# Attention and FP4 feed-forward on one core: the queue's products as two halves of 64 rows between the scores

## The chip, the core and the metric

The kernel runs on one core of a Trainium2 chip. The core has a matrix engine (TensorE, "PE" in the profile, with its weight loads shown apart as "PEld"), VectorE ("DVE"), ScalarE ("ACT"), GpSimd ("POOL") and SyncE ("SP"), whose queue issues nearly all of the transfers here. TensorE writes only to PSUM, which has eight banks of 512 float32 columns for each of its 128 partitions. The metric is the device time of one execution in microseconds (us), as a median of runs.

## The reference

One transformer layer with layer norms behind its two blocks, on x of 4 x 2048 x 256 in float32. Attention has 16 heads of 16 elements. The feed-forward block quantizes its inputs and weights to FP4 (E2M1) in blocks of 16 and has 704 hidden units.

```python
q, k, v = (split_heads(x @ W.T) for W in (Wq, Wk, Wv))
attn = softmax(einsum('bhld,bhmd->bhlm', q, k) * SCALE, axis=-1)
x = layernorm(x + merge_heads(einsum('bhlm,bhmd->bhld', attn, v)) @ Wo.T)

def fp4_quant_dequant(x):            # blocks of 16 along the last dimension
    scale = maximum(max(abs(xb)) / 6.0, 1e-12)
    idx = searchsorted(_MID, abs(xb / scale))
    return _GRID[idx] * sign(xb) * scale

def fp4_linear(x, w):
    return einsum('bsk,nk->bsn', fp4_quant_dequant(x), fp4_quant_dequant(w))

h = silu(fp4_linear(x, w_gate)) * fp4_linear(x, w_up)
x = layernorm(x + fp4_linear(h, w_down))
```

## The kernel before

**Steps and periods.** A step is one batch, one block of 512 queries and one group of four heads: 4 x 4 x 4 = 64 steps. Each step has 16 key tiles of 128 keys, and the main loop at the end of `block_kernel` runs one *period* for each key tile of each step, 1024 in all. A period does four heads' worth of three things on TensorE:

- `maxima` (scores for the row maxima, 20 periods ahead of the exponentials): two pairs of score matmuls into `pm`, each pair a tile of two banks. VectorE reduces each pair in one instruction of 1024 elements per partition (L397).
- `exponentials`: two pairs of score matmuls into `pe`, one bank for each head; ScalarE takes the exponential of each (L431).
- `values` (two periods behind the exponentials): four matmuls of 32 output columns each into the bank `av`, one for each head.

A score contracts 62 or 64 rows. The q and k of a pair of heads lie on partitions 0 to 63 (`j` = 0) and 64 to 127 (`j` = 1), so the two matmuls of a pair use different rows of the array. The order within a period is: both pairs of `maxima`, the first pair of `exponentials`, `values`, the second pair of `exponentials`, and then the period's part of the queue.

**The queue.** All other work is written as generators that yield after each part. `period` takes one such part for each period (`urgent` ones first): projections (`project`), the turning of maxima into rows (`max_rows`), the division by the sums (`normalize`), and for each block of 512 rows a `chain` through `feed_forward`: `residual`, the gate and up products (`gated`), transposes (`turned`) and `down`. A part is a group of matmuls on all 128 rows into one bank from `psum`, and its eviction by ScalarE. By shape there are four kinds: four transposes of 128 x 128; products of two contraction chunks with up to 256 output columns (pq, pv, py) or with 352 (pg, pu); and `down`'s products of six chunks (the last of 64 rows) with 128 columns (pz). A float32 matmul call stands in the profile as two matmul records, a score or a transpose as one.

**PSUM.** `ps_m` holds two tiles of two banks for `pm`; `ps_x` holds three banks that `pe` and the queue's parts share; one bank is `av`.

**Helpers.** `later` and `take_due` put VectorE's and GpSimd's work a given number of periods later. `fp4` quantizes a tile in two such steps: reduce, scale, reciprocal and the first multiplication at once, then the rounding. `layer_norm` issues all of its instructions at once. `load_k` fills a ring of 20 key tiles (two for each 512 keys of a step), 28 periods ahead of the exponentials and 8 ahead of the maxima.

**Order.** TensorE's instructions are kept in the order of the code (L134 and L137 are the helpers that record it). Every engine works through its instructions as written, each waiting for the semaphores of what it needs.

Of the kernel before, what the change touches and what calls it, by code (L numbers as in the profile page):

```python
# [30 lines left out]
F32 = mybir.dt.float32  # L32
# [21 lines left out]
LAG = 2  # L54
LEAST = 300.0
# [9 lines left out]
EXPONENT = 0x7F800000  # L65

# [7 lines left out]
def block_kernel(  # L74
# [24 lines left out]
    ps_m = ctx.enter_context(tc.tile_pool(name="ps_m", bufs=2, space=PSUM))  # L99
    ps_av = ctx.enter_context(tc.tile_pool(name="ps_av", bufs=1, space=PSUM))  # L100
    ps_x = ctx.enter_context(tc.tile_pool(name="ps_x", bufs=3, space=PSUM))


    banks = {"n": 0, "more": False}

    def psum(name):
        banks["n"] += 1
        if banks["more"] and banks["n"] % 2:
            return ps_m.tile([P, 2, 512], F32, tag="pm", name=name)[:, 0, :]
        return ps_x.tile([P, 512], F32, tag="px", name=name)  # L110
# [5 lines left out]
    def later(periods, step, rest=0):  # L116

        state = {"done": None}
        due.append((clock["now"] + periods, step, state))
        return lambda: state["done"] is not None and clock["now"] >= state["done"] + rest  # L120

    def take_due():
        clock["now"] += 1
        for _ in range(len(due)):
            at, step, state = due.popleft()
            if at > clock["now"]:
                due.append((at, step, state))
                continue
            step()
            state["done"] = clock["now"]  # L130


    def matmul(*args, **kw):
        tc.keep_in_program_order(nc.tensor.matmul(*args, **kw))  # L134

    def transpose(*args):
        tc.keep_in_program_order(nc.tensor.transpose(*args))  # L137
# [7 lines left out]
    def fp4(pool, t, tag, gain=1.0, engine=None):  # L145

        p, nb, _ = t.shape
        amax = pool.tile([p, nb], F32, tag="amax" + tag, name="amax")
        nc.vector.tensor_reduce(amax, t, AX.X, ALU.max, apply_absolute_value=True)  # L149
        sc = pool.tile([p, nb], F32, tag="sc" + tag, name="sc")  # L150
        nc.vector.tensor_scalar(sc, amax, gain / 6.0, 1e-12, ALU.mult, ALU.max)
        rs = pool.tile([p, nb], F32, tag="rs" + tag, name="rs")
        nc.vector.reciprocal(rs, sc)
        engine = engine or nc.gpsimd
        engine.tensor_scalar(rs, rs, gain * TIES_DOWN, 1.0, ALU.mult, ALU.mult)
        xn = pool.tile([p, nb, FB], F32, tag="xn" + tag, name="xn", bufs=3 if tag else 2)
        engine.tensor_tensor(xn, t, rs.unsqueeze(2).to_broadcast([p, nb, FB]), ALU.mult)

        def rounded():
            m = pool.tile([p, nb, FB], F32, tag="m" + tag, name="m", bufs=1)  # L160
            nc.vector.tensor_single_scalar(m.bitcast(I32), xn.bitcast(I32), EXPONENT, ALU.bitwise_and)
            nc.vector.tensor_scalar(m, m, 1.0, ROUND, ALU.max, ALU.mult)  # L162
            engine.tensor_tensor(xn, xn, m, ALU.add)  # L163
            engine.tensor_tensor(xn, xn, m, ALU.subtract)  # L164
            engine.tensor_tensor(xn, xn, sc.unsqueeze(2).to_broadcast([p, nb, FB]), ALU.mult)  # L165

        return xn, later(1, rounded, 4 if tag == "" else 2)
# [37 lines left out]
    for name, w in (("wk", wk), ("wq", wq), ("wv", wv)):  # L205
        loaded[name] = p2.tile([P, KC, D], F32, tag="xnh", name=name, bufs=3)
# [7 lines left out]
    for name, dst in (("wk", wkT), ("wq", wqT), ("wv", wvT)):  # L214
        for kc in range(KC):
            pt = psum("ptw")
            for n in range(KC):
                transpose(pt[:, n * P : (n + 1) * P], loaded[name][:, n, kc * P : (kc + 1) * P], ident)
            if name == "wv":
# [9 lines left out]

    RF = FF // 8  # L230

    def prepare():
# [5 lines left out]
        for kc in range(KC):  # L238
            for n in range(KC):
                at = (kc * KC + n) * P  # L240
                transpose(pt[:, at : at + P], raw[:, n, kc * P : (kc + 1) * P], ident)
        nc.scalar.copy(woT.rearrange("p k n -> p (k n)"), pt)
        yield 500

        def load(w, i):
            if w is w_down:
                t = p2.tile([P, FF], F32, tag="wl", name="wl", bufs=1)
                nc.sync.dma_start(t, w[i * P : (i + 1) * P, :])
                return fp4(p2, t.rearrange("p (b f) -> p b f", f=FB), "h")
            t = p2.tile([RF, 2, D], F32, tag="wl", name="wl", bufs=1)  # L250
            nc.sync.dma_start(t, w[2 * i * RF : 2 * (i + 1) * RF, :].rearrange("(c p) k -> p c k", p=RF))
            return fp4(p2, t.rearrange("p c (b f) -> p (c b) f", f=FB), "")

        def transposed(w, i, q, done):
            while not done():
                yield LEAST
            if w is w_down:
                q = q.rearrange("p b f -> p (b f)")
                for c0 in range(0, NFC, 4):
                    pt = psum("ptw")  # L260
                    for c in range(c0, min(c0 + 4, NFC)):
                        n = min(P, FF - c * P)
                        at = (c - c0) * P
                        transpose(pt[:n, at : at + P], q[:, c * P : c * P + n], ident)
                        nc.scalar.copy(wdT[:n, c, i * P : (i + 1) * P], pt[:n, at : at + P])
                return
            q = q.rearrange("p (c b) f -> p c (b f)", c=2)
            pt = psum("ptw")
            for kc in range(KC):
                for c in range(2):  # L270
                    at = (2 * kc + c) * RF
                    transpose(pt[:, at : at + RF], q[:, c, kc * P : (kc + 1) * P], ident[:RF, :RF])
# [3 lines left out]
            )  # L276

        pieces = [(w, i) for w in (w_gate, w_up) for i in range(4)] + [(w_down, i) for i in range(KC)]
        q = load(*pieces[0])
        yield 1  # L280
        for piece, after in zip(pieces, pieces[1:] + [None]):
# [3 lines left out]
            yield 500  # L285

    def weave(main, other, k):

        for cost in main:
            yield cost  # L290
            for _ in range(k if cost else 0):
                cost = next(other, None)
                if cost is None:
                    break
                yield cost
# [4 lines left out]
    def project(b, tb, what):  # L300
# [7 lines left out]
        for kc in range(KC):  # L308
            pt = psum("ptx")
            for t in range(QT):  # L310
                transpose(pt[:, t * P : (t + 1) * P], xb[:, t, kc * P : (kc + 1) * P], ident)
            nc.scalar.copy(xT[:, kc, :], pt)
            yield 600
        for name, c in [(w[0], int(w[1])) for w in what if w != "v"]:
# [3 lines left out]
            for half in range(2):  # L318
                cols = slice(half * QB // 2, (half + 1) * QB // 2)
                pq = psum("pq")[:, : QB // 2]  # L320
                for kc in range(KC):
                    matmul(pq, w[:, kc, c * P : (c + 1) * P], xT[:, kc, cols], start=(kc == 0), stop=(kc == KC - 1))
                nc.scalar.copy(hi[:, cols], pq)
                nc.gpsimd.tensor_tensor(lo[:, cols], read(pq), hi[:, cols].bitcast(F32), ALU.subtract)
                yield 900
# [7 lines left out]
        for t in range(QT if "v" in what else 0):  # L333
            v = vt[t // 2]
            pv = psum("pv")
            for kc in range(KC):
                matmul(
                    pv[:, :D], xT[:, kc, t * P : (t + 1) * P], wvT[:, kc, :], start=(kc == 0), stop=(kc == KC - 1)
                )
            src = pv[:, :D].rearrange("p (g i j d) -> p g i j d", g=NG, i=NP, j=2)  # L340
            for j in range(2):
                nc.scalar.copy(v[:, :, t % 2, :, 2 * j * DH : (2 * j + 1) * DH], src[:, :, :, j, :])
            if t % 2:
                t0 = tb * QT + t - 1
                for g in range(NG):
                    nc.sync.dma_start(vx[b % 2][g, :, t0 : t0 + 2, :], v[:, g].rearrange("p t i c -> p t (i c)"))
            if t == QT - 1:
                projected.add((b, tb, "v"))
            yield 900
# [15 lines left out]
    def load_k(s, kb):  # L365
        b, qb, g = steps[s]
        for i in range(NP):
            c, h = divmod(g * HG + i * 2, NC)
            k = p1.tile([P, QB], F32R, tag="k", name="k", bufs=20)
# [12 lines left out]
    def maxima(s, n, i):  # L382

        if n == 0 and i == 0:
            mx_sb[s] = p2.tile([P, QT, HG, NQB], F32, tag="mx", name="mx")
        kb, t = n // QT, n % QT
        pm = ps_m.tile([P, 2, QB], F32, tag="pm", name="pm")
        for j in range(2):
# [386 lines left out]
```

## Time and profile before

The three runs took 3696.54, 3698.85 and 3699.21 us (median 3698.85). The profiled execution took 3695.37 us, with a span of 3693.6 us from its first to its last instruction; its mean granted TensorE clock was 0.982.

| what | busy us | share of the span | instructions |
|---|---|---|---|
| TensorE matmuls (PE) | 3540.7 | 96% | 21396 |
| TensorE weight loads (PEld) | 1602.0 | 43% | 21396 |
| VectorE (DVE) | 2805.0 | 76% | 3250 |
| ScalarE (ACT) | 2694.0 | 73% | 5452 |
| GpSimd (POOL) | 1293.4 | 35% | 1542 |

"Busy" is the time in which at least one instruction of the engine was under way, so a TensorE that is busy is not one that has both halves of its rows at work. The 16 DMA engines moved 334.18 MB at 90 GB/s on average. The first group of `values` starts at 125.6 us and the last at 3598.4 us; the periods of the main loop lie between, the preparation before, and the last block's feed-forward behind.

A row of the timeline gives the start and the time from the first start to the last end of a run of like instructions, both in us; `x4` counts instructions, and brackets show idle time and what ended it. A row of a group gives busy time and the mean of one in ns, then the idle time before them. Start-to-start times in the timeline are the safer reading for matmuls, because their ends are modelled.

### The profile page before, as it was taken

The page shows a single profiled execution, that of the slowest core. Times are in us where ns is not written, and L with a number is a line of the kernel's source. Part 1 is how long each engine was busy: PE and PEld are TensorE (multiplying, and loading weights), DVE is VectorE, ACT ScalarE, POOL GpSimd, SP SyncE. Part 2 cuts the span into 40 slices and gives each one's busy share as a digit, 9 for nine tenths or more (in the row PEclk, how much of TensorE's full clock was granted, in tenths as well). Part 3 has the DMA queues.
Part 4 walks back from the last instruction along what each step waited for, and adds up shares of the span by engine and source line. Part 5 has one row for each costly group of instructions (what it writes and reads, how often), then busy time and mean ns, then how long its engine had stood idle before and what let it go on. Part 6 is the DMA issues. An engine that isn't in the chain of part 4 may idle for free.

```text
span 3693.6 us, 57860 instructions
## 1 busy us (share of the span) xinstructions
PE 3540.7 (96%) x21396; PEld 1602.0 (43%) x21396; DVE 2805.0 (76%) x3250; ACT 2694.0 (73%) x5452; POOL 1293.4 (35%) x1542
## 2 busy tenths in 40 slices
PE   5889999999999999999999999999999999999995
PEld 4433444444444444444444444444443434444343
DVE  3777777787787877878787787778778788878834
ACT  2667777777777777777777777777777777777772
POOL 0331432424243242423424243342424325241425
PEclk8899999999999999999999999999999999999997
DMA  6643333223232332323323232322322221222100
GB/s 217 188 137 117 93 91 105 81 85 115 68 114 84 94 94 85 109 70 109 95 78 106 85 97 88 97 89 74 113 75 63 75 79 57 75 68 86 47 7 6
DMA packets 197954, 334.18 MB, mean 90 GB/s; under 512 B 26024, under 2 KB 75560, under 8 KB 197672
## 3 DMA queue, kind: packets, MB, share of 16 engines
q1 hardware_dynamic: 196280, 329.16, 29.2%
q8 instruction: 171, 2.80, 0.3%
q10 hardware_dynamic: 1392, 1.31, 0.1%
q14 instruction: 111, 0.91, 0.1%
HBM read 242.81 MB, written 86.51 MB: 89 GB/s over the span
## 4 chain that ended last, share of the span: by engine, by line
PE 82%; DVE 11%; DMA 2%; POOL 2%; SPq 1%; issue 1%; ACT 1%; ACTq 0%; POOLq 0%; DVEq 0%
PE av L134 24%; PE pe L134 18%; PE pm L134 16%; DVE mx L397 8%; PE pz L134 5%; PE pg L134 5%; PE pu L134 5%; PE pq L134 3%; PE pth L137 1%; PE pv L134 1%; PE pa L137 1%; PE py L134 1%; PE pn L137 1%; DMA k<-kx 1%; DMA xb<-in_L_attn_x_dram 1%; DVE amax L149 1%
## 5 line engine op out<-in xcount | busy, mean ns | idle before, releaser
L397 DVE TENSOR_REDUCE mx<-pm 128x2 f32<-128x1024 f32 x2048 | 2407.9, 1217 | 706.8 <-PE pm L134 702.5
L431 ACT ACTIVATE e<-pe 128x512 f32<-128x512 f32 x4096 | 2217.9, 595 | 671.2 <-PE pe L134 666.0
L134 PE MATMUL av<-e,v 128*32 128x512 f32 x8192 | 1098.3, 608 | 0.0
L134 PE MATMUL pe<-q,k 64*128 64x512 f32 x4096 | 1037.2, 456 | 4.8 <-ACT e L431 4.4
L134 PEld LDWEIGHTS pe<-q,k 64*128 64x128 f32 x4096 | 476.4, 185 | 969.0 <-ACT e L431 855.7
L134 PE MATMUL pm<-k,q 62*128 62x512 f32 x4096 | 803.8, 448 | 60.0 <-DVE mx L397 53.0
L134 PEld LDWEIGHTS pm<-k,q 62*128 62x128 f32 x4096 | 347.0, 186 | 373.2 <-issue 178.6
L134 PEld LDWEIGHTS av<-e,v 128*32 128x32 f32 x8192 | 162.2, 108 | 332.2 <-issue 314.1
L537 POOL TENSOR_TENSOR a<-a,g 128x352 f32<-128x352 f32 x124 | 116.4, 939 | 499.5 <-ACT a L536 499.5
L582 POOL TENSOR_TENSOR x<-x,read 128x128 f32<-128x128 f32 x128 | 58.9, 460 | 493.6 <-ACT read L142 493.6
L134 PE MATMUL pz<-wdT,hT 128*128 128x128 f32 (+1 forms) x1536 | 230.0, 292 | 0.0
L163 POOL TENSOR_TENSOR xn<-xn,m 128x704 f32<-128x704 f32 (+2 forms) x104 | 159.5, 1534 | 157.7 <-DVE m L162 139.0
L134 PEld LDWEIGHTS pz<-wdT,hT 128*128 128x128 f32 (+1 forms) x1536 | 191.0, 191 | 45.5 <-ACT e L431 18.2
L551 POOL TENSOR_TENSOR h<-a,u 128x352 f32<-128x352 f32 x124 | 116.2, 937 | 226.7 <-ACT u L550 224.4
L134 PE MATMUL pg<-wgT,xqT 128*128 128x352 f32 x512 | 187.4, 489 | 0.0
L513 POOL TENSOR_TENSOR x<-x,read 128x256 f32<-128x256 f32 x64 | 46.7, 730 | 400.2 <-ACT read L142 399.9
L134 PE MATMUL pu<-wuT,xqT 128*128 128x352 f32 x512 | 186.1, 486 | 0.0
L164 POOL TENSOR_TENSOR xn<-xn,m 128x704 f32<-128x704 f32 (+2 forms) x104 | 159.8, 1536 | 5.6
L165 POOL TENSOR_TENSOR xn<-xn,sc 128x704 f32<-128x704 f32 (+2 forms) x104 | 131.5, 1264 | 7.8
L538 POOL TENSOR_TENSOR a<-a,g 128x352 f32<-128x352 f32 x124 | 118.8, 958 | 9.7
L134 PEld LDWEIGHTS pg<-wgT,xqT 128*128 128x128 f32 x512 | 88.3, 191 | 58.5 <-ACT e L431 19.1
L134 PEld LDWEIGHTS pu<-wuT,xqT 128*128 128x128 f32 x512 | 88.2, 191 | 58.7 <-ACT e L431 20.0
(95 smaller groups left out, 2283.1 us busy)
## 6 DMA issues: line engine op xcount, KB each, us to landing
k<-kx SPq DMA_DIRECT2D x1024, 128.0 KB
v<-vx SPq DMA_DIRECT2D x64, 768.0 KB
q<-qx SPq DMA_DIRECT2D x256, 124.0 KB
kx<-khi SPq DMA_DIRECT2D x64, 256.0 KB
qx<-qhi SPq DMA_DIRECT2D x64, 256.0 KB
xb<-in_L_attn_x_dram SPq DMA_DIRECT2D x27, 512.0 KB
vx<-vt SPq DMA_DIRECT2D x128, 96.0 KB
x<-in_L_attn_x_dram SPq DMA_DIRECT2D x16, 512.0 KB
```

The lines of the kernel that those rows point to most:

```text
L134: tc.keep_in_program_order(nc.tensor.matmul(*args, **kw))
L137: tc.keep_in_program_order(nc.tensor.transpose(*args))
L163: engine.tensor_tensor(xn, xn, m, ALU.add)
L164: engine.tensor_tensor(xn, xn, m, ALU.subtract)
L165: engine.tensor_tensor(xn, xn, sc.unsqueeze(2).to_broadcast([p, nb, FB]), ALU.mult)
L397: nc.vector.tensor_reduce(mx_sb[s][:, t, 2 * i : 2 * i + 2, kb], pm, AX.X, ALU.max)
L431: nc.scalar.activation(e, pe[j], AF.Exp, scale=SCALE)
L513: nc.gpsimd.tensor_add(x1[:, t, :], x1[:, t, :], read(py[:, :D]))
L537: engine.tensor_mul(a, a, g)
L538: engine.tensor_add(a, a, g)
L551: engine.tensor_mul(h[:, cols], a, u)
L582: nc.gpsimd.tensor_add(x1[:, t, cols], x1[:, t, cols], read(pz))
```

## The change

Six things change together.

1. **Halves.** While the main loop has both maxima and exponentials (`split["on"]`), `product` cuts each product of the queue into matmuls on rows 64 to 127 (the part's `upper` ones) and matmuls on rows 0 to 63, which add up in the same bank. Transposes (`turn`) stay on all rows.
2. **Order.** A generator now yields a `Part` (a list of calls) before its eviction. The main loop issues the period's work by a table: `m` and `e` with a head's number are scores for maxima and for exponentials (heads 0 and 2 on rows 0 to 63, heads 1 and 3 on rows 64 to 127), `u` the upper half of the product, `l` its lower half and its eviction, `q` a transposing part and its eviction, `v` the values.
3. **Banks by head.** Maxima take one bank for each head, three in rotation, and VectorE reduces 512 elements in each of twice as many instructions. Four banks serve exponentials and the queue. A bank returns to its rotation when its last read has been issued.
4. **VectorE's steps.** `fp4` becomes four due steps in place of two (except for weights), and `layer_norm` one step for each of its tiles; their consumers wait some periods longer, and the gate products of all four row tiles now come before the first `turned`.
5. The tanh of the gate reads the copy in SBUF in place of PSUM.
6. **Rings.** Key tiles 16 in place of 20; exponentials' tiles 11 in place of 10; the quantized tiles `xn` of the hidden units 4 in place of 3.

```diff
+ORDER = {
+    "none": "e3 m1 m2 e1 v e2 m3 m0 e0",
+    "turn": "e1 m1 q m2 e3 e0 m3 v m0 e2",
+    "square": "u m0 e0 e2 m1 v e1 e3 m2 l m3",
+    "wide": "u m2 e2 m0 e0 v m1 e1 e3 l m3",
+    "long": "u e2 m2 m0 e0 v m3 e1 e3 l m1",
+}
...
+    banks, banks_m, taken = deque(range(4)), deque(range(4, 7)), {}
...
+    def product(out, pairs):
+        kind = "long" if len(pairs) > 2 else "wide" if out.shape[1] > QB // 2 else "square"
...
+        upper = rows(1) if split["on"] else []
+        parts = upper + rows(0) if split["on"] else pairs
+        calls = [
+            lambda n=n, lhsT=lhsT, rhs=rhs: matmul(out, lhsT, rhs, start=(n == 0), stop=(n == len(parts) - 1))
+            for n, (lhsT, rhs) in enumerate(parts)
+        ]
+        return Part(kind, calls, len(upper))
...
+        if spread:
+            done = later((wait, largest), (1, scaled), (2, power), (1, rounded), rest=3 if tag else 5)
...
-            k = p1.tile([P, QB], F32R, tag="k", name="k", bufs=20)
+            k = p1.tile([P, QB], F32R, tag="k", name="k", bufs=16)
...
-        pm = ps_m.tile([P, 2, QB], F32, tag="pm", name="pm")
-        for j in range(2):
-            rows = slice(R * j, R * j + RM)
-            matmul(
-                pm[:, j, :],
...
-        nc.vector.tensor_reduce(mx_sb[s][:, t, 2 * i : 2 * i + 2, kb], pm, AX.X, ALU.max)
+        rows = slice(R * j, R * j + RM)
+        bank = banks_m.popleft()
+        pm = bank_of(bank, "pm")
+        matmul(pm, q_sb[s, i][rows, t * P : (t + 1) * P], k_sb[s, i, kb][rows, :], start=True, stop=True)
+        nc.vector.tensor_reduce(mx_sb[s][:, t, h : h + 1, kb], pm, AX.X, ALU.max)
+        banks_m.append(bank)
...
-            nc.scalar.activation(a, pg[:, :FH], AF.Tanh, scale=0.5)
+            was_read("pg")
+            nc.scalar.activation(a, g, AF.Tanh, scale=0.5)
...
+            part, g = take_part()
+            for step in ORDER[part.kind if g else "none"].split():
+                if step == "v" and n >= LAG:
+                    values(n - LAG)
...
+                elif step == "u":
+                    for call in part[: part.upper]:
+                        call()
+                elif step in "ql" and g is not None:
+                    for call in part[part.upper :]:
+                        call()
+                    part_done(g)
+                elif step[0] == "m" and m < N:
+                    maximum(m * HG + int(step[1]))
+                elif step[0] == "e" and n < N:
+                    exponential(n * HG + int(step[1]))
```

## The prediction

> **What bounds the kernel now.** I read the page first (busy shares, the chain), then the stretches, then TensorE's timeline, period by period, and last VectorE's. From the page and the groups:
>
> ```profile
> PE 3540.7 (96%) x21396; PEld 1602.0 (43%) x21396; DVE 2805.0 (76%) x3250; ACT 2694.0 (73%) x5452; POOL 1293.4 (35%) x1542
> PE 82%; DVE 11%; DMA 2%; POOL 2%; SPq 1%; issue 1%; ACT 1%; ACTq 0%; POOLq 0%; DVEq 0%
> L397 DVE TENSOR_REDUCE mx<-pm 128x2 f32<-128x1024 f32 x2048 | 2407.9, 1217 | 706.8 <-PE pm L134 702.5
> L431 ACT ACTIVATE e<-pe 128x512 f32<-128x512 f32 x4096 | 2217.9, 595 | 671.2 <-PE pe L134 666.0
> L149 DVE TENSOR_REDUCE amax<-x 128x32 f32<-128x512 f32 x32 | 21.5, 672 | 4.1 <-POOL x L497 4.1
> ```
>
> VectorE and ScalarE have idle time, and TensorE ends most of it; TensorE is the bound. The timeline shows what one period spends: a square product (pq) first, a wide one (pg) next, a long one (pz) last.
>
> ```profile
> 1500.03 1.07 PE L134 MATMUL av<-e,v 128*32 128x512 f32 x8
> 1501.02 0.50 PE L134 MATMUL pe<-q,k 64*128 64x512 f32 x2
> 1501.45 1.13 PE L134 MATMUL pq<-xT,wqT 128*128 128x256 f32 x4
> 1502.51 0.74 PE L134 MATMUL pm<-k,q 62*128 62x512 f32 x4
> 1503.07 0.42 PE L134 MATMUL pe<-q,k 64*128 64x512 f32 x2
> 1503.42 1.07 PE L134 MATMUL av<-e,v 128*32 128x512 f32 x8
> ...
> 1508.04 0.66 PE L137 MATMUL ptq<-ident,xn 128*128 128x128 f32 x4
> 1508.62 0.73 PE L134 MATMUL pm<-k,q 62*128 62x512 f32 x4
> ...
> 1514.22 1.45 PE L134 MATMUL pg<-wgT,xqT 128*128 128x352 f32 x4
> 1515.61 0.73 PE L134 MATMUL pm<-k,q 62*128 62x512 f32 x4
> ```
>
> ```profile
> 1842.51 1.07 PE L134 MATMUL av<-e,v 128*32 128x512 f32 x8
> 1843.51 0.50 PE L134 MATMUL pe<-q,k 64*128 64x512 f32 x2
> 1843.94 1.69 PE L134 MATMUL pz<-wdT,hT 128*128 128x128 f32 x11
> 1845.26 0.50 PE L134 MATMUL pm<-k,q 62*128 62x512 f32 x1
> 1845.46 0.27 PE L134 MATMUL pz<-wdT,hT 64*128 64x128 f32 x1
> 1845.49 0.71 PE L134 MATMUL pm<-k,q 62*128 62x512 f32 x3
> 1845.84 0.60 PE L134 MATMUL pe<-q,k 64*128 64x512 f32 x2
> 1846.37 0.64 PE L134 MATMUL av<-e,v 128*32 128x512 f32 x4
> ```
>
> Start to start: values 0.99, one pair of scores 0.43, pq 1.06, two pairs of maxima 0.56, one pair 0.35; together 3.39 us. The wide period adds 1.39 - 1.06 and takes about 3.71, the long one 3.86 (1842.51 to 1846.37). A transposing period takes 3.09: its transposes are 0.58, its sum is 2.91, and the rest is waiting for a score's bank. Between the first and last values (125.6 to 3598.4 us) I counted 240 wide, 120 long, 217 square and 318 transposing periods; 127 had no part and took 351 us, 2.76 each.
>
> Two equations split the scores: one pair alone (between values and a product) is 0.43, three pairs in a row (0.56 + 0.35) are 0.91. So a pair costs 0.24, and entering and leaving its arrangement of the array 0.19. Without such a 0.19, a pass of a product costs (1.06 - 0.19)/4 = 0.22 with 256 columns and (1.39 - 0.19)/4 = 0.30 with 352. A long period leaves 3.86 - 0.99 - 0.43 - 0.91 = 1.53 for pz, so (1.53 - 0.19)/12 = 0.11 a pass.
>
> **Can half a product run beside scores?** That decides the sign. In the code each float32 call makes two passes, one behind the other, and `down`'s last chunk (64 rows, on 0 to 63) stands ahead of all the maxima. The rows at 1845 show otherwise (pz's x11 hold ten passes of 128 rows and the chunk's first): a maximum on the other 64 rows starts at 1845.26, ahead of the chunk's second pass at 1845.46, which precedes it in the code. Likewise eight values passes (four heads, two each) fit in 0.99 us: one head alone has two passes of 512 columns, so the four heads' first passes must start side by side, each past the waiting second passes of the heads ahead of it. The two halves of the rows act as two queues, also where one holds float32 products and the other scores.
>
> The Trainium skill says otherwise ("TensorE: Matmul & The Clock Gate", section "Step-by-step: what each phase is for"): "The MATMULs themselves stay in program order", and only weight loads are pulled ahead. By that rule the sum would be the 4200 us of the rival in program order; by the row at 1845.26 it is the sum that follows. The measured row decides.
>
> **Parts 1 and 2, halves and order.** A product cut in two needs twice the passes, each on half the rows: no array time is saved by itself. What goes is the product's own arrangement (0.19), and one entry of the scores (0.19). Between two groups of values each half now has four scores and one half of the products' passes, across the period's border:
> - square: 4 x 0.24 + 4 x 0.22 = 1.84, with 0.19 and 0.99: 3.02 instead of 3.39, 0.37 less; 217 x 0.37 = 80 us
> - wide: 0.96 + 4 x 0.30 = 2.16, with 1.18: 3.34 instead of 3.71; 240 x 0.37 = 89 us
> - long: 0.96 + 12 x 0.11 = 2.28, with 1.18: 3.46 instead of 3.86; 120 x 0.40 = 48 us
> - transposing: nothing is cut, and 2.91 remains; what can go is the wait for a bank, at most 3.09 - 2.91 = 0.18; 318 x 0.18 = 57 us, at least 0.
>
> Doubled weight loads lie beside the passes, as pz's do: a pass of 0.11 with a load for each. The best sum is 274 us less.
>
> **Part 3, banks by head.** VectorE's reductions become 4096 of 512 elements. Its timeline:
>
> ```profile
> 1889.21 3.46 DVE L397 TENSOR_REDUCE mx<-pm 128x2 f32<-128x1024 f32 x3
> ```
>
> Back to back, one of 1024 follows the last by (3.46 - 1.217)/2 = 1.12. A reduction of 512 is in the group of L149: 0.672, and 128x704 there is 0.876, so 1.06 ns an element. Back to back I get 1.12 - 0.512 x 1.06 = 0.58, alone 0.68. The rest of VectorE's work is (2805.0 - 2407.9)/1024 = 0.39 a period. So its need is 4 x 0.58 + 0.39 = 2.71 to 4 x 0.68 + 0.39 = 3.11, against (2 x 1.12 + 0.39) = 2.63 now. At 2.71 it stays below every period but the empty ones, which are at 2.76 already. At 3.11, square falls by 0.28 only (61 us), transposing rises by 0.02 (-6) and empty by 0.35 (-44): 61 + 89 + 48 - 6 - 44 = 148 us less. Single banks free each bank sooner; and three maxima banks hold three heads where two tiles held four. I take 250 of 274 to 148: nearer the first, since reductions do run back to back when VectorE is short, and less than all, since VectorE is now within 10% of the square and transposing periods. ScalarE needs 4 x 0.595 + (2694.0 - 2217.9)/1024 = 2.84 at most, below 2.91.
>
> In the order, each `m` waits for VectorE and each `e` for ScalarE, and what is behind it on TensorE's queue waits too, the other half's passes included. With three and four banks that bites only if VectorE lags by three heads (1.7 us); I cost it in the 24 us between 274 and 250, and its upper end is the second rival.
>
> **The rest.** Parts 4 and 6 lengthen the feed-forward chain by some periods; empty periods (127) and the next block's projections cover it. Without that cover, an empty period takes work from none: the number of periods is fixed, and at the end the lag is in rounds without work; 0, bounds -5 to +10. The last 95 us behind 3598.4 keep whole products and gain banks: -5 to +5. The preparation up to 125.6 us waits for loads: 0, -5 to +10. Part 5: GpSimd's first step waits for tanh as before; 0. With 16 key tiles, `load_k` waits on SP for the exponentials of the period before, where 20 let it be three groups earlier; behind it in SP's queue are the maxima's rows, the stores and later loads. The maxima need these tiles eight periods later, some 25 us, and four issues took 4.98 us in the timeline at 1501.23. I cost it at 0; with the cover gone, a late group of tiles would show as TensorE waiting for k, at up to 1 us in each of 64 steps: 64. `layer_norm`'s pieces issue the same instructions.
>
> Sum against the profiled execution: 3695.4 - 250 = 3445 us. It stands 3.5 us below the median of the runs, 0.1%, which I leave. A difference under 0.2% can't be told from none here.
>
> **Rivals.**
> - *Program order holds* (slower). If a half waits for all that precedes it, `u` runs nearly alone, then the lower scores. Square: e1 0, e3 and m2 0.24, `l` from 0.48, m3 at its last pass 1.14, u 1.38 to its last pass 2.04, three lower scores to 2.76; with 1.18 that is 3.94, 0.55 more. Wide in the same way 3.48 + 1.18 = 4.66, 0.95 more; long 5.06, 1.20 more; transposing 3.15. Sum 119 + 228 + 144 + 19 = 510: about 4200 us. Against it is the row at 1845.26. For it: there only one pass waited, while `u` has 4 in a wide product and 10 in a long one. Values show a fourth head's pass going past three waiting ones and their loads, which is what a wide product's `u` asks (one pass running, three waiting). It decides from the point where three waiting passes can't be passed: wide periods then cost 240 x 1.32 = 317 us, more than the whole gain. If only long ones fail, 120 x 1.60 = 192 us are lost: 3640.
> - *VectorE becomes the bound* at 0.68 a head: 3695 - 148 = 3547 us; with waits spreading to the other half up to 3620. For it: 2.71 to 3.11 against 2.9 to 3.0. Against: three rows in 3.46 us.
> - *No change.* If the saved switches return as bank waits, 0.37 a product: about 3695. For it: `pe` waits for ScalarE's banks, 0.18 a transposing period. Against: a fourth bank, and products that now take nothing out of the scores' time.
>
> **How the numbers follow.** Halves at work with VectorE nearly hidden 0.60 (3360 to 3510), VectorE as the bound 0.26 (3510 to 3640), no change 0.04, program order 0.10. The prediction is the first, 3445. Its own range is 3360 to 3510; the range given, 3360 to 3620, takes in the VectorE rival and leaves out the last two and the tails. Faster 0.87, same 0.03, slower 0.10.
>
> **What would show it.** In the changed profile: scores beside `pq`, `pg` and `pz` in the same stretch and values starting every 3.0 (square), 3.35 (wide), 3.45 (long) and 2.9 us (transposing); a reduction of 512 at 0.58 to 0.68, with VectorE busy near 90% of the span; ScalarE near 80%; no TensorE wait for k. Wide periods over 4 us would mean program order; periods of all kinds near 3.1, with TensorE waiting for `mx`, would mean VectorE.

## The result, and the profile after

The changed kernel takes 3846.61 us (median of 4 runs, 3840.40 to 3857.93); the kernel before, beside it on the same chip, takes 3697.69. The ratio is 1.0406 (95% interval 1.0385 to 1.0427): 149 us slower, where the prediction had 250 us less. The profiled execution took 3840.40 us with a span of 3838.6; the first values start at 131.9 us and the last at 3745.8. The preparation is 6 us longer and what follows the last values 2 us shorter, so 141 of the 145 us between the two profiled executions lie in the main loop.

The page of the changed kernel: busy time, the shares of the chain that ended last, and the group of VectorE's reductions (busy time and mean ns of one, idle time before and what ended most of it).

```profile
PE 3599.6 (94%) x24344; PEld 1885.6 (49%) x24344; DVE 3011.8 (78%) x5298; ACT 2651.7 (69%) x5452; POOL 1286.6 (34%) x1542
PE 71%; POOL 9%; DVE 9%; issue 6%; DMA 3%; ACT 2%; SPq 0%; POOLq 0%; ACTq 0%
L496 DVE TENSOR_REDUCE mx<-pm 128x1 f32<-128x512 f32 x4096 | 2636.8, 683 | 498.1 <-PE pm L164 223.2
```

TensorE has 82% of the chain before and 71% now; GpSimd has gone from 2% to 9%, though its busy time has not grown. No engine has become the bound by its amount of work. The halves themselves run beside the scores. TensorE's timeline of a wide product (start, duration, tile, records in the row):

```profile
1815.10 1.06 PE L164 MATMUL av<-e,v 128*32 128x512 f32 x8
1816.10 0.50 PE L164 MATMUL pm<-k,q 62*128 62x512 f32 x1
1816.11 0.56 PE L164 MATMUL pg<-wgT,xqT 64*128 64x352 f32 x1
1816.44 0.39 PE L164 MATMUL pe<-q,k 64*128 64x512 f32 x1
1816.51 0.46 PE L164 MATMUL pg<-wgT,xqT 64*128 64x352 f32 x1
...
1818.43 1.07 PE L164 MATMUL av<-e,v 128*32 128x512 f32 x8
```

A pass of the product on 64 rows every 0.30 us and, between them, scores on the other 64 rows: from values to values 3.33 us, where the same period took 3.71 before. From values to values, by kind, as the median of the starts in the trace (the prediction's 2.76 for an empty period was a mean):

| period | before | predicted | after |
|---|---|---|---|
| square, between two square ones | 3.39 | 3.02 | 3.10 |
| wide, between two wide ones | 3.71 | 3.34 | 3.33 |
| long | 3.86 | 3.46 | 4.16 |
| transposing, by itself | 3.09 | 2.91 | 2.92 |
| empty | 2.65 | 2.76 | 2.74 |
| a wide and a transposing one together | 6.80 | 6.25 | 6.93 (4.33 + 2.60) |

So long periods are slower, the border to a transposing period takes no less, and some periods stand still: a `pq` period of 4.63 and one of 5.38 us follow each other. There VectorE's timeline reads (the bracket: idle time before, and what ended it):

```profile
1832.94 0.89 DVE L218 TENSOR_REDUCE amax<-h 128x44 f32<-128x704 f32 x1 [1.09 <-POOL h L652]
1833.74 1.28 DVE L496 TENSOR_REDUCE mx<-pm 128x1 f32<-128x512 f32 x2
...
1835.15 0.43 DVE L225 RECIPROCAL rs<-sc 128x44 f32<-128x44 f32 x1
1835.49 0.63 DVE L496 TENSOR_REDUCE mx<-pm 128x1 f32<-128x512 f32 x1
1837.40 1.04 DVE L233 TENSOR_SCALAR m<-xn 128x704 int32<-128x704 int32 x1 [1.28 <-POOL xn L228]
1838.36 0.68 DVE L496 TENSOR_REDUCE mx<-pm 128x1 f32<-128x512 f32 x1
1838.96 0.51 DVE L238 TENSOR_SCALAR m<-m 128x704 f32<-128x704 f32 x1
1839.39 3.77 DVE L496 TENSOR_REDUCE mx<-pm 128x1 f32<-128x512 f32 x6
```

GpSimd's and TensorE's rows of the same stretch:

```profile
1835.67 0.23 POOL L226 TENSOR_SCALAR rs<-rs 128x44 f32<-128x44 f32 x1 [2.76 <-DVE rs L225]
1835.98 1.39 POOL L228 TENSOR_TENSOR xn<-h,rs 128x704 f32<-128x704 f32 x1
```

```profile
1836.60 1.06 PE L164 MATMUL av<-e,v 128*32 128x512 f32 x8
1837.60 0.73 PE L164 MATMUL pe<-q,k 64*128 64x512 f32 x2
1839.09 0.49 PE L164 MATMUL pm<-k,q 62*128 62x512 f32 x1 [0.76 <-DVE mx L496]
```

VectorE first waits 1.09 us for GpSimd's `h` (L218). Then `fp4`'s power step (`m<-xn`, L233) stands only one reduction behind the reciprocal, though the code puts two periods, eight reductions, between them. GpSimd needs 0.23 and 1.39 us for what the step reads. VectorE waits 1.28 us for it, the maxima behind it stay unread, all three maxima banks fill, and TensorE stops until a reduction ends at 1839.04, with `pq`'s half and all else queued behind that `m`. Then six reductions run in 3.77 us.

The order of the code is not the order that VectorE got. The text ahead of the prediction said that every engine works through its instructions as written; VectorE did not get them as written. The framework's scheduler may place an engine's instructions in another order than the code's, unless they are recorded with `keep_in_program_order`, which this code does for TensorE alone. (By what measure it places them no run shows.) In the trace of the changed kernel 92 of 106 power steps stand one or two reductions of a maximum behind the reciprocal.

From the list of waits of the changed kernel (in total us, times, longest):

```profile
PEld pm L164 <- DVE mx L496: 760.7, 1000, 7.3
DVE m L233 <- POOL xn L228: 88.5, 86, 3.8
DVE st L597 <- POOL x L680: 63.1, 32, 16.3
DVE amax L218 <- POOL h L652: 52.1, 33, 14.5
DVE amax L218 <- POOL x L607: 43.7, 32, 2.2
DVE st L597 <- POOL x L622: 29.5, 33, 3.4
```

VectorE stands waiting for GpSimd for 277 us by its last five rows. The same five waits of the kernel before sum to 71 us (30.0, 17.1, 12.9, 7.2 and 4.1).

### The profile page after: what moved, and what is told of

It reads as the page before. It is cut to its first block, busy times and chain, and to the rows that moved or that the text cites. A ratio compares the mean times of both kernels' runs of the same rounds, so it can differ in the third digit from the quotient of the medians.

```text
span 3838.6 us, 66273 instructions
## 1 busy us (share of the span) xinstructions
PE 3599.6 (94%) x24344; PEld 1885.6 (49%) x24344; DVE 3011.8 (78%) x5298; ACT 2651.7 (69%) x5452; POOL 1286.6 (34%) x1542
## 4 chain that ended last, share of the span: by engine, by line
PE 71%; POOL 9%; DVE 9%; issue 6%; DMA 3%; ACT 2%; SPq 0%; POOLq 0%; ACTq 0%
PE av L164 21%; PE pm L164 17%; PE pe L164 13%; PE pz L164 6%; DVE mx L496 5%; PE pg L164 3%; PE pu L164 3%; POOL xn L228 2%; PE pq L164 2%; DVE m L233 2%; ACT e L535 1%; PE pth L167 1%; PE pv L164 1%; DMA k<-kx 1%; POOL h L652 1%
## 5 line engine op out<-in xcount | busy, mean ns | idle before, releaser
L496 DVE TENSOR_REDUCE mx<-pm 128x1 f32<-128x512 f32 x4096 | 2636.8, 683 | 498.1 <-PE pm L164 223.2
L164 PE MATMUL pm<-k,q 62*128 62x512 f32 x4096 | 1753.9, 470 | 158.4 <-DVE mx L496 142.1
L164 PE MATMUL pe<-q,k 64*128 64x512 f32 x4096 | 1518.4, 432 | 0.0
L164 PEld LDWEIGHTS pm<-k,q 62*128 62x128 f32 x4096 | 731.7, 188 | 925.0 <-DVE mx L496 760.7
L164 PEld LDWEIGHTS pe<-q,k 64*128 64x128 f32 x4096 | 711.3, 188 | 423.1 <-ACT e L535 340.2
L164 PE MATMUL pg<-wgT,xqT 64*128 64x352 f32 (+1 forms) x992 | 351.6, 474 | 0.0
L164 PE MATMUL pu<-wuT,xqT 64*128 64x352 f32 (+1 forms) x988 | 350.6, 475 | 0.0
L164 PE MATMUL pz<-wdT,hT 64*128 64x128 f32 (+1 forms) x2656 | 336.9, 280 | 0.0
L164 PEld LDWEIGHTS pz<-wdT,hT 64*128 64x128 f32 (+1 forms) x2656 | 304.5, 189 | 6.1 <-issue 3.8
L164 PEld LDWEIGHTS pu<-wuT,xqT 64*128 64x128 f32 (+1 forms) x988 | 173.5, 187 | 18.0 <-issue 0.4
L233 DVE TENSOR_SCALAR m<-xn 128x704 int32<-128x704 int32 (+2 forms) x106 | 73.6, 695 | 88.9 <-POOL xn L228 88.5
```

The lines of the kernel that those rows point to most:

```text
L164: return tc.keep_in_program_order(nc.tensor.matmul(*args, **kw))
L233: nc.vector.tensor_single_scalar(m.bitcast(I32), made[2].bitcast(I32), EXPONENT, ALU.bitwise_and)
L496: nc.vector.tensor_reduce(mx_sb[s][:, t, h : h + 1, kb], pm, AX.X, ALU.max)
```

## The experiments

Two theories stood at the start. **V**: VectorE's steps that need GpSimd stand too early in its queue, and the reductions behind them fill the three banks. **R**: a half of a long product (ten or twelve passes) is too much waiting work for TensorE to reach the scores behind it. The rival was that halves are worth nothing, or cost time. All times are medians; each ratio is to the kernel before on the same chip, with its 95% interval.

**VectorE in the order of the code.** Each `nc.vector` call goes through a wrapper.

```diff
+    class InOrder:
+        def __init__(self, engine):
+            self.engine = engine
+        def __getattr__(self, name):
+            f = getattr(self.engine, name)
+            return lambda *a, **k: tc.keep_in_program_order(f(*a, **k))
+    VE = InOrder(nc.vector)
...
-        nc.vector.tensor_reduce(mx_sb[s][:, t, h : h + 1, kb], pm, AX.X, ALU.max)
+        VE.tensor_reduce(mx_sb[s][:, t, h : h + 1, kb], pm, AX.X, ALU.max)
```

> The changed kernel with VectorE's instructions issued in the order in which the code places them; before this they are placed by the planner's own estimate, and only TensorE is held to the code. Theory V (VectorE's quantizing and norm steps wait for GpSimd, the maxima's reductions stand behind them, three maxima banks fill and TensorE waits): in the code's order two periods' reductions stand between xn and the step that needs it, so the 277 us that VectorE waits for GpSimd fall below 100 and the time falls by 150 to 250 us, to 3600 to 3700. Theory R (TensorE's reach is too short for the ten to twelve passes of a long product): no change, 3847, since the long periods stay at 4.16 us.

3603.19 us, ratio 0.9746 (0.9729 to 0.9762): 243 us less than the changed kernel, and faster than the kernel before. In its trace VectorE's rows carry the wrapper's line, L117:

```profile
1760.84 0.43 DVE L117 RECIPROCAL rs<-sc 128x44 f32<-128x44 f32 x1
1761.18 1.88 DVE L117 TENSOR_REDUCE mx<-pm 128x1 f32<-128x512 f32 x3
1763.36 0.69 DVE L117 TENSOR_REDUCE mx<-pm 128x1 f32<-128x512 f32 x1 [0.30 <-PE pu L174]
1764.29 2.10 DVE L117 TENSOR_REDUCE mx<-pm 128x1 f32<-128x512 f32 x3 [0.24 <-PE pe L174]
1766.69 0.69 DVE L117 TENSOR_REDUCE mx<-pm 128x1 f32<-128x512 f32 x1 [0.31 <-PE pg L174]
...
1767.98 0.52 DVE L117 TENSOR_SCALAR m<-xn 128x704 int32<-128x704 int32 x1
```

Eight reductions now lie between the reciprocal and the power step, which finds its operand ready and takes 0.52 us. Stretches of over 4.55 us from values to values are 10, where the changed kernel has 120 and the kernel before 7. That distance is eight in 88 of 106 cases here. Long periods are still 4.16 us, so what was gained is V's and not R's.

**Only the three steps that wait for GpSimd.** To tell their place from that of all other VectorE work, only `amax`, the power step and `bn_stats` are held; the reductions of the maxima and the rest are placed by the scheduler.

```diff
-            nc.vector.tensor_reduce(amax, t, AX.X, ALU.max, apply_absolute_value=True)
+            tc.keep_in_program_order(nc.vector.tensor_reduce(amax, t, AX.X, ALU.max, apply_absolute_value=True))
...
-            nc.vector.tensor_single_scalar(m.bitcast(I32), made[2].bitcast(I32), EXPONENT, ALU.bitwise_and)
+            tc.keep_in_program_order(
+                nc.vector.tensor_single_scalar(m.bitcast(I32), made[2].bitcast(I32), EXPONENT, ALU.bitwise_and)
+            )
...
-            nc.vector.bn_stats(st, r[:, t0 + t, :])
+            tc.keep_in_program_order(nc.vector.bn_stats(st, r[:, t0 + t, :]))
```

> The changed kernel as it is, but with three VectorE instructions held behind all that the code places before them: the block maxima (amax), the power step (m from xn) and the norm's statistics (st), which are the ones that waited for GpSimd. All else on VectorE stays where the planner puts it, and long products stay in a row. If it is the early place of these three that costs: 3600 to 3650, most of the 243 us that holding all of VectorE gave. If other steps' places matter as much (the turning of maxima, the division by the sums, the reductions among themselves): 3700 to 3847.

3609.95 us, ratio 0.9765 (0.9749 to 0.9781): 237 of the 243 us. From its waits, to be set beside those of the changed kernel:

```profile
PEld pm L164 <- DVE mx L498: 533.5, 871, 2.9
DVE st L599 <- POOL x L682: 50.7, 6, 16.3
DVE m L234 <- POOL xn L228: 10.6, 13, 1.8
DVE amax L218 <- POOL h L654: 4.8, 1, 4.8
```

The row of the power step falls from 88.5 us to 10.6, that of `amax<-h` from 52.1 to 4.8; the longest wait of TensorE for a maxima bank falls from 7.3 to 2.9 us. The early place of these three steps is the cause; V is shown.

Part of the price may come by way of TensorE's clock. In the changed kernel from 400 us to the last values there are 21 stretches of 3.4 or 6.8 us with a granted clock of 0.50, each within 2 us of the end of a stop of TensorE of 1.2 to 2.7 us. At one of them VectorE has waited 1.32 us for GpSimd's `x` (L607), waits again for `xn`, and TensorE stops for 2.06 us. The first two rows are TensorE's; the third is the stretch behind the stop, with the busy times of PE, PEld, DVE, ACT and POOL and then the clock:

```profile
1983.54 0.79 PE L164 MATMUL pm<-k,q 62*128 62x512 f32 x1 [2.06 <-DVE mx L496]
1984.26 1.93 PE L164 MATMUL av<-e,v 128*32 128x512 f32 x8
```

```profile
1983.60:1990.30 6.70, 6.70 (x25) 3.42 (x27) 5.34 (x10) 2.36 (x5) 3.68 (x4) 0.50 0.00 0
```

The values take 1.93 us instead of 1.06. The 21 stretches sum to 113 us; in the runs with VectorE in order and with the three steps held there are none from 400 us on. The mean clock of the profiled executions is 0.970 in the changed kernel and 0.985 with VectorE in order, so an estimate of what the clock takes of the 243 us is 0.030 x 3838.6 - 0.015 x 3601.3 = 61 us, if TensorE is what everything waits for in these stretches. That the stops bring the lower clock is read from their standing together; no run changed one without the other.

**The same order in the kernel before.** Is the order of the code simply better? The wrapper, in the kernel before:

```diff
-        nc.vector.tensor_reduce(amax, t, AX.X, ALU.max, apply_absolute_value=True)
+        VE.tensor_reduce(amax, t, AX.X, ALU.max, apply_absolute_value=True)
```

(and so for every other VectorE instruction)

> The kernel before with VectorE's instructions in the code's order. Theory V: there VectorE waits for GpSimd only 71 us in all and TensorE is the bound of each period, so within 20 us of 3697. If the planner's order costs in any kernel, whatever its slack: 3500 to 3620.

3740.56 us, ratio 1.0116 (1.0101 to 1.0131): 43 us slower, which neither theory had. A likely reason, not tried by itself: the code of the kernel before issues its steps in lumps and leaves GpSimd little room, and there the scheduler does better. The code's order paid in the changed kernel and cost time in the kernel before.

**The steps as before.** Part 4 undone, the scheduler's order kept:

```diff
-        if spread:
-            done = later((wait, largest), (1, scaled), (2, power), (1, rounded), rest=3 if tag else 5)
-        else:
-            done = later(
-                (wait, lambda: (largest(), scaled())), (1, lambda: (power(), rounded())), rest=2 if tag else 4
-            )
+        done = later(
+            (wait, lambda: (largest(), scaled())), (1, lambda: (power(), rounded())), rest=2 if tag else 4
+        )
...
-        later(*[(1, lambda t=t: moments(t)) for t in range(n)], (0, normal))
+        for t in range(n):
+            moments(t)
+        normal()
```

with the shorter distances in `feed_forward` that went with it.

> The changed kernel without part 4: the quantizing in two steps, the norms at once, the gate products and the first turn in the order of before; halves, order and banks stay as changed. If it is the spreading of the steps that lets VectorE wait for GpSimd: the 277 us of such waits fall towards the 71 us of before and the time by 100 to 200 us, to 3650 to 3750. If it is the shorter slack (three maxima banks, shorter periods) and not the steps: within 40 us of 3847. Theory R: no change.

3969.23 us, ratio 1.0734 (1.0718 to 1.0750): 123 us slower than the changed kernel, outside both ranges. So part 4 is not what made the change slow; it is worth 123 us even in the scheduler's order, and what it lacks is that its distances reach VectorE's queue. The five waits for GpSimd did not fall towards 71 us but rose to 313, that of the power step to 99.7, where the kernel before, with the same two steps, has 12.9. In the kernel before 87 of 106 power steps stand two reductions of 1024 behind the reciprocal, here 74 stand one reduction of 512 behind it.

**Long halves in pieces.** `U` and `L` stand for the next two calls (four passes) of the half on the upper or lower rows, with scores of the other rows between them.

```diff
-    "long": "u e2 m2 m0 e0 v m3 e1 e3 l m1",
+    "long": "U m2 U m0 U e2 e0 v m3 e1 e3 L m1 L l",
```

> The changed kernel with the long products' halves issued in pieces of two calls (four passes) between the scores, in place of ten and twelve passes in a row. Theory R: no score then stands behind more than about three waiting passes, and a long period falls from 4.16 to about 3.5 us; 120 of them make 80 us less, about 3770. Theory V: no change, 3847.

3796.74 us, ratio 1.0269 (1.0254 to 1.0285): 50 us less than the changed kernel, and long periods of 3.47 us instead of 4.16. What stood in the way is seen in TensorE's rows and its weight loads. First the changed kernel, its matmuls and then its loads in a long period:

```profile
1917.32 0.60 PE L164 MATMUL pz<-wdT,hT 64*128 64x128 f32 x3
...
1917.76 0.38 PE L164 MATMUL pz<-wdT,hT 64*128 64x128 f32 x2
...
1917.98 0.61 PE L164 MATMUL pz<-wdT,hT 64*128 64x128 f32 x4
1918.32 0.50 PE L164 MATMUL pm<-k,q 62*128 62x512 f32 x1
1918.43 1.17 PE L164 MATMUL pz<-wdT,hT 64*128 64x128 f32 x10
1919.33 0.50 PE L164 MATMUL pe<-q,k 64*128 64x512 f32 x1
```

```profile
1917.76 0.75 PEld L164 LDWEIGHTS pz<-wdT,hT 64*128 64x128 f32 x6
1918.32 0.18 PEld L164 LDWEIGHTS pm<-k,q 62*128 62x128 f32 x1
1918.43 1.09 PEld L164 LDWEIGHTS pz<-wdT,hT 64*128 64x128 f32 x10
1919.33 0.18 PEld L164 LDWEIGHTS pe<-q,k 64*128 64x128 f32 x1
```

The lower half has twelve passes, the `pm` at 1918.32 stands behind them in the queue, and its load comes only when nine of them (3 + 2 + 4) have started. The upper half has ten; the `pe` at 1919.33 comes when seven of these have started (ten in the row, three of them the lower half's last). So in all 78 stretches between two long products: a score enters past three waiting passes with their loads, not past four. The scores that should lie beside a long half come when it is nearly done. With pieces of four passes (this timeline is of the next experiment, which has the same pieces):

```profile
1777.85 1.07 PE L174 MATMUL av<-e,v 128*32 128x512 f32 x8
1778.84 0.49 PE L174 MATMUL pm<-k,q 62*128 62x512 f32 x1
1778.85 0.49 PE L174 MATMUL pz<-wdT,hT 64*128 64x128 f32 x2
1779.18 0.40 PE L174 MATMUL pe<-q,k 64*128 64x512 f32 x1
1779.18 0.50 PE L174 MATMUL pz<-wdT,hT 64*128 64x128 f32 x3
...
1781.32 1.06 PE L174 MATMUL av<-e,v 128*32 128x512 f32 x8
```

3.47 us from values to values: R is shown for the long products.

**Both together.** The wrapper and the pieces.

> The changed kernel with both repairs: VectorE in the code's order and the long products in pieces. If the two causes are separate, the gains add: 243 us for the order and 50 us for the pieces off 3847, 3553. The long periods were shortened by 0.68 us in the median (4.155 to 3.472), which is 80 us in 120 periods, so up to 3525 if the pieces gave less before only because VectorE's waits took it back. If the long periods then wait for VectorE instead: 3590 to 3603.

3541.61 us, ratio 0.9575 (0.9559 to 0.9591). The two gains add: 243 and, on top of it, 62 (alone it was 50). This is 156 us faster than the kernel before; stretches over 4.55 us have gone from 120 to 11.

**Whole products.** To price the halves, the changed kernel without the split, all kinds of period with one order.

```diff
 ORDER = {
+    kind: "m0 m1 m2 m3 e0 e1 v e2 e3 l" for kind in ("none", "turn", "square", "wide", "long")
 }
...
-        split["on"] = 0 <= n and m < N
+        split["on"] = False
```

> The changed kernel without parts 1 and 2: products whole, and the order of the kernel before (all maxima, two exponentials, values, two exponentials, the part). Banks by head, VectorE's steps and the rings stay as changed. If the halves and the order save what the square and wide periods show (3.10 and 3.33 in place of 3.39 and 3.71), these return to the old lengths and the time is not below the changed kernel's by more than the long periods' 4.16 to 3.86, 36 us: 3810 to 3950. If the halves themselves are the loss: 3700. Theory V expects the steps' loss to stay in part, so above 3740.

4703.45 us, ratio 1.2725 (1.2686 to 1.2764), which none of the theories had. The order is the likely main cause: four maxima in a row need four banks, and there are three.

```profile
2003.59 0.73 PE L160 MATMUL pm<-k,q 62*128 62x512 f32 x3
2004.88 0.49 PE L160 MATMUL pm<-k,q 62*128 62x512 f32 x1 [0.56 <-DVE mx L492]
```

The fourth `pm` waits until VectorE has read the first; TensorE's `pm` waited so 1017 times. The run prices three banks with a bad order, not the halves. So the same once more, with VectorE in the order of the code (as in the first experiment) and the maxima in two pairs:

```diff
-    kind: "m0 m1 m2 m3 e0 e1 v e2 e3 l" for kind in ("none", "turn", "square", "wide", "long")
+    kind: "m0 m1 e0 e1 v m2 m3 e2 e3 l" for kind in ("none", "turn", "square", "wide", "long")
```

> The changed kernel with VectorE in the code's order, but products whole, in an order that three maxima banks can serve: two maxima, two exponentials, values, two maxima, two exponentials, the part (the run with four maxima in a row made TensorE wait for VectorE in each period). Halves and their order are then the only difference to the run with VectorE in order, 3603. If the halves save the product's own arrangement of the array: square periods at 3.39, wide ones at 3.71, long ones at 3.86, and 3680 to 3740, so the halves are worth 80 to 140 us. If the gain over the kernel before came from the banks by head and VectorE's order: 3603 to 3640.

3774.67 us, ratio 1.0206 (1.0190 to 1.0221). That is 929 us less than the run before, of which VectorE's order may account for some 240. Against the first experiment, which differs by the halves and the order of every kind of period, it is 171 us slower; its wide periods take 3.72 and its square ones 3.39 us, as in the kernel before, where halves take 3.33 and 3.11. The 171 us are not the price of the halves alone: transposing periods, which hold no halves, take 3.34 us among themselves in this run's one order and 2.98 in the first experiment, and empty ones 2.95 and 2.74. What the halves are worth is better seen in the wide and square periods than in this total.

**ScalarE in the order of the code too**, on top of both together:

```diff
+    SE = InOrder(nc.scalar)
...
-        nc.scalar.activation(e, pe, AF.Exp, scale=SCALE)
+        SE.activation(e, pe, AF.Exp, scale=SCALE)
```

> As the run with both repairs, and ScalarE's instructions in the code's order as well. TensorE's loads for the exponentials waited 374 us for ScalarE in the run with VectorE in order. If the planner puts evictions ahead of exponentials and that is what is waited for: 20 to 60 us less than with both repairs. If it is the four banks and ScalarE's pace: the same within 10 us.

3537.00 us, ratio 0.9566 (0.9552 to 0.9581), the fastest of all; 5 us less than without, where the intervals of the ratios overlap. ScalarE's order is not where time is lost.

**Another order for the transposing period.** In both together, a product's period and a transposing one behind it take 4.33 and 2.60 us (71 pairs with a wide product, medians), where the prediction has 6.25 for the two. The stretch of 4.33 holds ten scores. The order was changed to bring the transposes forward:

```diff
-    "turn": "e1 m1 q m2 e3 e0 m3 v m0 e2",
+    "turn": "m1 q e1 m2 e3 e0 m3 m0 v e2",
```

> The kernel with both repairs (3541.6), with another order in transposing periods: m1 q e1 m2 e3 e0 m3 m0 v e2, which puts one score ahead of the transposes and one behind the values in place of two and two. In the kernel with both repairs a wide period and the transposing one behind it took 4.27 + 2.60 = 6.87 us where the prediction has 6.25, with six scores on rows 64 to 127 in one stretch beside four passes on the others. If that unevenness at the borders is where the rest of the predicted gain went: 0.24 us for each transposing period between products, some 120 to 150 of 318, 30 to 36 us less, about 3508. If these periods wait for VectorE or for banks: the same, or slower.

3595.94 us, ratio 0.9728 (0.9713 to 0.9742): 54 us slower. The second stretch became shorter (2.38 us) but the first longer (4.66): it now holds six maxima, which at 0.62 us a reduction are 3.7 us of VectorE, on three banks (a reading that was not tried). Most of the 54 us lies elsewhere: the 187 stretches that hold transposes and no product sum to 660 us instead of 603, and behind an empty period one takes 3.94 instead of 3.34. And with ScalarE's order held as well:

> As the run with the other transposing order, and ScalarE in the code's order as well, which gave 4.6 us with both repairs alone. If the two are separate: about 3503 to 3537, that is, 5 us below the run with the other order.

3598.95 us, ratio 0.9733 (0.9719 to 0.9748): no different. The wide pair takes 4.66 + 2.38 = 7.04 us where it took 6.93, so what the border costs was not won back.

## Why the prediction was wrong, and where it was right

The miss is 3847 - 3445 = 402 us. By the runs, 243 of it are VectorE's queue, 62 the long halves (the second on top of the first), and 97 are left (3542 - 3445).

- **The failed step: the price of TensorE's wait for VectorE. An `m` that waits for VectorE "bites only if VectorE lags by three heads (1.7 us); I cost it in the 24 us between 274 and 250".** In the scheduler's order it cost 243 us instead of 24, 237 of them by the place of three steps. The threshold fits the stop shown: between 1836.12 and 1838.36 us no reduction runs, 2.24 us, and TensorE stands still for 0.76. That it would be reached so often (120 stretches from values to values are over 4.55 us, against 7 before) was missed, since the steps were taken to stand where the code puts them. "The rest" costs part 4 at 0 on the same ground; undoing part 4 made the kernel 123 us slower, so the part itself is not the loss. What the step left out is the chain VectorE, GpSimd, VectorE inside `fp4` and `layer_norm`: a step placed one or two reductions (0.62 to 1.24 us) behind the reciprocal waits for 1.6 us of GpSimd. The kernel before shows the same wait for 13 us only: there the two instructions between are reductions of 1024 elements, 2.24 us together, which cover the 1.6. Reductions of half the size took that cover away. That reading is argued from the traces; the run with the steps as before agrees with it (99.7 us of this wait behind reductions of 512). The prediction also took the clock to stay as it was; by the estimate above the lower clock next to the longest stops may have 61 of the 243 us.
- **The second miss is the size of a half.** The rival in program order named the point from which it decides, "where three waiting passes can't be passed", and gave 192 us if only the long products fail. Three are passed and a fourth is not, so the long products fail and the others do not. That case had no chance of its own beside the rival's 0.10, and its size was put too high, since the scores come past the last three: 120 x (4.16 - 3.46) = 84 us by the periods, 50 and 62 by the runs.
- **Halves side by side: right.** The row at 1845.26 of the kernel before carried over to four passes: 3.33 us measured for 3.34. The Trainium skill's rule that was weighed there ("TensorE: Matmul & The Clock Gate", section "Step-by-step: what each phase is for": the matmuls stay in program order) does not hold for scores on the other rows, by the wide and square periods; past a fourth waiting pass it holds, by the long ones. The sum it gave, 4200, was 353 us too high.
- **Costs of VectorE: right.** A reduction takes 0.683 us in the mean and (3.77 - 0.683)/5 = 0.62 back to back, for 0.68 and 0.58. It has not become the bound by its need: in the version with both edits it is busy for 2992.8 of 3541.6 us, 85%. In the changed kernel it shows 78% and ScalarE 69%, not 90% and 80%; the span is longer, and the work is what was said.
- **Square periods** take 3.10 instead of 3.02: 217 x 0.08 = 17 us of the 97. Where the 0.08 goes was not tried.
- **The border between a product and transposes** was not in the sum at all: each period was counted as if its own halves were even. In the version with both edits 71 wide pairs exceed their two predicted periods by 4.33 + 2.60 - 6.25 = 0.68 us, 44 square ones by 4.09 + 2.37 - 5.93 = 0.53, and 18 long ones by nothing: 48 + 23 = 71 us, by medians. With the 17 us, and a preparation that is 9 us longer in that version than before (134.1 for 125.6), this adds up to the 97; since the sum had held back 24 us for VectorE besides, as much again is unexplained. Why the border costs this is argued only: of the ten scores of the long stretch eight lie on the upper rows and two on the lower, beside a half product there, so that one half of the array is short of work; and scores in it start up to 0.57 us apart where 0.24 is the pace elsewhere, which a wait for a bank would give. The two runs that turned the order do not settle it.
- **Three costs of 0 held.** TensorE waits for a key tile once, for 6 us, with the smaller ring; the preparation is 6 us longer; what lies behind the last values is 2 us shorter.

## What to carry to other kernels

Where a framework places an engine's instructions itself, a distance written in the code is none until the trace shows it: count, in the timeline, what stands between a step and the one that feeds it on another engine, and hold those few steps in order (three instructions were worth 237 us here). When instructions that cover a round trip to another engine become shorter, price that round trip against the new cover. When work is to run beside other work on one in-order queue, cut it into pieces no longer than the engine's reach past waiting instructions, and measure that reach in the smallest and the largest case, not in one.

## What was not expected of the hardware

TensorE starts a matmul on one half of its rows ahead of earlier ones that wait on the other half, though the instructions are in one queue; its reach was three waiting passes with their loads in 78 of 78 stretches between long products (4.16 us in one row, 3.47 in pieces of four). In the changed kernel 21 stretches of 3.4 or 6.8 us with a granted clock of 0.50 stood within 2 us of a stop of TensorE of 1.2 to 2.7 us. And with three banks of maxima the loss around two stalls of VectorE was larger than the stalls: they were 1.09 and 1.28 us, and the periods around took 4.63 and 5.38 us, 3.6 more than a square and a wide one (3.10 and 3.33).
